# Gathers into one tile, weighted sums behind the attention heads, and PSUM copies pinned to ScalarE, in a two-layer recurrent, mixture-of-experts and attention kernel

## The chip, the cores and the metric

The kernel runs as one program on 1 core of one Trainium2 chip. The metric is the time of the execution on the device in microseconds, the median over several runs. Short names: PE is TensorE (PEld its weight loads), DVE is VectorE, ACT is ScalarE, POOL is GpSimd, SP is SyncE, which here only issues DMAs.

## The reference, cut to what matters

The input has 8 batches of 512 tokens with 128 channels, 4096 tokens in all. Everything is float32. Two layers follow each other, and each is `x + s * silu(g)` with two branches `s` and `g` over the same layer-normed input.

```python
# layer 0
xn = layernorm(x)
s  = mamba(xn) -> rmsnorm(+xn) -> gelu MLP -> rmsnorm          # scan over 512 tokens, 256 channels x 16 states
g  = silu(layernorm(moe24(relu(layernorm(moe24(xn)))) + xn))   # 24 experts, top-2, two passes
x  = x + s * g
# layer 1
xn = layernorm(x)
s  = attention(xn)        # 8 heads, causal over 512 tokens, head width 128
e1, e2 = top2(softmax(xn @ wg))                   # 128 experts, at most 32 rows each
yb = rows of xn sorted by expert @ we             # 2 x 4096 rows of 128
y  = w1[:, None] * yb[row1] + w2[:, None] * yb[row2]
x  = x + s * silu(y)
```

The last four lines matter most here. The second mixture of experts needs the routing of all 8 batches before its first expert can run, and every token then fetches two rows of the table `yb`, weights them and adds them.

## The kernel before

The work is written as Python generators, and the framework puts the instructions of each engine into a fixed order when the program is built. It goes by its own model of times and by the data dependences. Each engine then runs its list strictly in order. Semaphores make it wait for the other engines.

**Stage A (to about 690 us).** The first mixture of experts runs (`expert1`, `between`, `expert2`), interleaved with the first batches of the state-space model. One batch of the model is `front`, 8 steps of `scan` with 2 states each, `gate`, `gated` and `back`. The scan is DVE work: `L665` multiplies, `L667` is the scan proper and `L668` multiplies again. ACT makes `da` (`L663`), PE sums the products by transposing them into `py` (`L689`).

**Stage B (about 690 to 1309 us).** The attention of batches 0 to 5 (`EARLY = 6`) runs head by head beside the remaining batches of the model; the loop spreads the model's steps evenly over the 48 heads. For batch `b`, `fetch(b)` loads the layer-0 branches and adds gathered expert rows on POOL, and `after(b)` makes the input of layer 1: layernorm, a weight and a bias (`L605`, `L606`), silu (`L607`), times `s` (`L608`), plus `x` (`L609`). `prepare(b)` makes the transposed input `xaT`; `choose(b)` and `route(b)` rank the experts and scatter rows into `xs_dram` (`L896`).

One head is `probabilities` and then `values`. PE multiplies (`L914`, `L922`), DVE masks and takes the minimum (`L924`), ACT takes the exponential (`L928`), PE transposes the probabilities into one PSUM tile `pp` with a single buffer (`L942`), a copy takes them to `pT` in SBUF (`L944`), PE multiplies with `v` (`L949`) and DVE divides by the row sum and adds to `s1` (`L954`, `L958`, `L960`). The ten 128x128 blocks of a head go through `pp` in three groups: two of 128x384 and one of 128x512. Before heads 0 and 4 of a batch, `values_of` makes `v` for four heads: PE multiplies, and four copies of 128x512 bring it from PSUM (`L908`). Both kinds of copy are written for either engine:

```python
nc.any.tensor_copy(v[:, j, :, 0:D], pv)                      # L908
nc.any.tensor_copy(pT[:, first : first + n, :], pp[:, :n, :])  # L944
```

With `nc.any` the framework picks DVE or ACT for each copy when it builds the program.

**Stage C (about 1309 to 1400 us).** `back(7)` ends the model: the last `s`, in the tile `xo` (named `xnb` in the trace), is stored to `s_dram` (`L763`). `fetch(7)` loads it again as `sb` (`L583`), and `after(7)`, `prepare(7)`, `choose(7)` follow. The pools of the late stages (`psl`, `r3`, `mo`) are opened ahead of `after(7)`.

**Stage D (about 1400 to 1457 us).** `slots(t)` loads the sorted rows and transposes them into `xsT` (`L1025`, `L1028`, `L1030`), and `experts(e0)` multiplies them (`L1041`), masks them (`L1043`) and stores them to `yb_dram` (`L1044`). These steps are interleaved with the 16 late heads of batches 6 and 7 through the list `second`.

**Stage E (about 1457 us to the end).** `finish(b)` gathers two rows for each token from `yb_dram`: 8 indirect DMAs of 128 rows for a batch, 64 in all, issued by POOL (`L129`), into small tiles `ya`, `yc` with 6 buffers. DVE weights and adds them (`L1058`, `L1059`), ACT takes silu (`L1060`), DVE multiplies with the attention result `s1f` (`L1061`), adds `x1f` (`L1062`), and SP stores the batch. `finish(0)` to `finish(5)` stand in the list between the remaining heads, `finish(6)` and `finish(7)` behind them.

Of the kernel before, what the change touches and what calls it, by code (L numbers as in the profile page):

```python
# [8 lines left out]
F32 = mybir.dt.float32  # L9
# [11 lines left out]
P = 128  # L21
# [26 lines left out]
def tile_kernel(ctx: ExitStack, tc: tile.TileContext, t: dict, out: bass.AP):  # L48
# [94 lines left out]
    def rows(ap):  # L143

        return ap.rearrange("(j p) d -> p j d", p=P)
# [414 lines left out]
    def expert2(e, w):  # L560
# [14 lines left out]
            S.activation(os[:r, c, :], po[:r, c, :], AF.Copy, scale=wsl[:r, c, e : e + 1])  # L575
        store(os_dram, e, os)

    def fetch(b):

        o = af.tile([P, NJ, D], F32, name="o", bufs=2)  # L580
        Q.dma_start(o, rows(xn_dram[b * L : (b + 1) * L, :]))
        sb = af.tile([P, NJ, D], F32, name="sb")
        Q.dma_start(sb, rows(s_dram[b][:, :]))  # L583
# [12 lines left out]
        return o, sb, xb, o2  # L596

    def after(b, o, sb, xb, o2):

        E = G  # L600
        if o2 is not None:
            E = V
            V.tensor_tensor(o, o, o2, ALU.add)
        layernorm(st, o, o, NJ, eps6, "lno")
        E.tensor_tensor(o, o, bc(lno_w.unsqueeze(1), (P, NJ, D)), ALU.mult)  # L605
        E.tensor_tensor(o, o, bc(lno_b.unsqueeze(1), (P, NJ, D)), ALU.add)  # L606
        S.activation(o, o, AF.Silu)  # L607
        E.tensor_tensor(o, o, sb, ALU.mult)  # L608
        E.tensor_tensor(xb, o, xb, ALU.add)  # L609
        Q.dma_start(rows(x1_dram[b][:, :]), xb)  # L610
        return xb
# [111 lines left out]
    def back(b, yt):  # L723

        yz = mb.tile([P, 2, L], F32, name="yz")
        for hf in range(2):
            pt = ps_m.tile([P, L], F32, name="pyz", tag="pm")
            for i in range(NJ):
                T.transpose(pt[:, i * P : (i + 1) * P], yt[:, i, hf * P : (hf + 1) * P], ident)
            S.copy(yz[:, hf, :], pt)  # L730
        xo = mb.tile([P, NJ, D], F32, name="xnb")
        Q.dma_start(xo, rows(xn_dram[b * L : (b + 1) * L, :]))
        pr = ps_m.tile([P, NJ, D], F32, name="pr", tag="pm")
        for j in range(NJ):
# [28 lines left out]
        Q.dma_start(rows(s_dram[b][:, :]), xo)  # L763
        yield


# [35 lines left out]
    class Attention:  # L802
# [97 lines left out]
        def values_of(self, xaT, c):  # L900

            ps_q, pq = self.ps_q
            v = self.at.tile([P, NJ, 4, D + 1], F32, name="v", bufs=3)
            G.memset(v[:, :, :, D : D + 1], 1.0)
            for j in range(NJ):
                pv = ps_q.tile([P, 4, D], F32, name="pv1", tag=pq)
                T.matmul(pv, xaT[:, j * P : (j + 1) * P], self.w_vo[:, 4 * c : 4 * c + 4, :], start=True, stop=True)
                nc.any.tensor_copy(v[:, j, :, 0:D], pv)  # L908
            return v

        def probabilities(self, xaT, hd):
# [20 lines left out]
        def values(self, hd, prob, v, s1):  # L932
            at, (ps_t, pt), (ps_o, tpo) = self.at, self.ps_t, self.ps_o
            pT = at.tile([P, 10, P], F32, name="pT", bufs=2)
            for group in ((0, 1), (2,), (3,)):
                first = group[0] * (group[0] + 1) // 2
                n = sum(i + 1 for i in group)
                pp = ps_t.tile([P, NJ, P], F32, name="pp", tag=pt)
                c = 0
                for i in group:  # L940
                    for k in range(i + 1):
                        T.transpose(pp[:, c, :], prob[i][:, k * P : (k + 1) * P], ident)  # L942
                        c += 1
                nc.any.tensor_copy(pT[:, first : first + n, :], pp[:, :n, :])  # L944
            for i0 in range(0, NJ, 2):
                po = ps_o.tile([P, 2, D + 1], F32, name="po1", tag=tpo)
                for i in range(i0, i0 + 2):
                    for k in range(i + 1):
                        T.matmul(  # L949
                            po[:, i - i0, :], pT[:, i * (i + 1) // 2 + k, :], v[:, k, hd % 4, :],  # L950
                            start=(k == 0), stop=(k == i),
                        )
                rs = st.tile([P, 2], F32, name="rsum", bufs=4)
                V.reciprocal(rs, po[:, :, D])  # L954
                for i in range(i0, i0 + 2):
                    so, r = s1[:, i, :], rs[:, i - i0 : i - i0 + 1]
                    if hd == 0:
                        V.tensor_scalar(so, po[:, i - i0, 0:D], r, None, ALU.mult)  # L958
                    else:
                        V.scalar_tensor_tensor(so, po[:, i - i0, 0:D], r, so, ALU.mult, ALU.add)  # L960

        def heads(self, b, xaT):
            s1 = self.at.tile([P, NJ, D], F32, name="s1", bufs=2)
# [79 lines left out]
        V.tensor_tensor(yb, py, bc(live[:, e0 // 2 : e0 // 2 + 4].unsqueeze(2), (P, 4, D)), ALU.mult)  # L1043
        Q.dma_start(rows(yb_dram[2 * C1 * e0 : 2 * C1 * (e0 + 8), :]), yb)  # L1044

    def finish(b):
        s1 = mo.tile([P, NJ, D], F32, name="s1f")
        Q.dma_start(s1, rows(s1_dram[b][:, :]))
        x1 = mo.tile([P, NJ, D], F32, name="x1f")
        Q.dma_start(x1, rows(x1_dram[b][:, :]))  # L1050
        y = mo.tile([P, NJ, D], F32, name="y", tag="y")
        for j in range(NJ):
            i = b * NJ + j
            ya = mo.tile([P, D], F32, name="ya", tag="row", bufs=6)
            yc = mo.tile([P, D], F32, name="yc", tag="row", bufs=6)
            gather(ya, yb_dram, row1[:, i, 0:1])
            gather(yc, yb_dram, row1[:, i, 1:2])
            V.tensor_scalar(ya, ya, w121[:, i, 0:1], None, ALU.mult)  # L1058
            V.scalar_tensor_tensor(y[:, j, :], yc, w121[:, i, 1:2], ya, ALU.mult, ALU.add)  # L1059
        S.activation(y, y, AF.Silu)  # L1060
        V.tensor_tensor(y, y, s1, ALU.mult)  # L1061
        V.tensor_tensor(y, y, x1, ALU.add)  # L1062
        Q.dma_start(rows(out[b * L : (b + 1) * L, :]), y)


# [12 lines left out]
    def model():  # L1078
# [6 lines left out]
        for b in range(B):  # L1085
# [9 lines left out]
            for k in range(DS // NC):  # L1095
# [4 lines left out]
                    next(ending, None)  # L1100
                if k in (4, 5):
                    state = next(coming, None)
                if k == 6:
                    zsb = gate(xT)
                yield
            py, zs = pyb, zsb
# [72 lines left out]
        pass  # L1179
    for _ in attention_steps:  # L1180
        pass
    psc.close()
    ssm.close()

# [9 lines left out]
    xsT = r3.tile([P, E1, 2, C1], F32, name="xsT")  # L1194
    live = r3.tile([P, E1 // 2], F32, name="live")
    loaded = {e0: load_experts(e0) for e0 in range(0, 32, 8)}
    last = Attention(at, m_qk, w_vo, (ps_x, "px"), (ps_q, "pq"), (ps_s, "ps"), (ps_t, "pt"), (ps_o, "po"))
    for b in range(EARLY + 1, B):
        ready[b] = last.prepare(b, after(b, *fetch(b)))
        last.choose(b)  # L1200
    weights2()
    places()
# [12 lines left out]
    for t16 in range(E1 // 16):  # L1215
        second.append([lambda t16=t16: run_experts(t16)])
        if t16 + 1 < E1 // 16:
            second[-1].append(lambda t16=t16: slots(t16 + 1))
    for b in range(EARLY):
        second.append([lambda b=b: finish(b)])  # L1220
    for _ in late():
        for f in second.pop(0) if second else []:
            f()
    for f in sum(second, []):
        f()
    for b in range(EARLY, B):
        finish(b)
    psl.close()
    atc.close()

# [63 lines left out]
```

## Time and profile before

| what | value |
|---|---|
| time, median of 7 runs (lowest to highest) | 1554.15 us (1545.77 to 1561.83) |
| the profiled execution: its time, its span | 1553.7 us, 1552.0 us |
| mean granted TensorE clock | 0.894 |
| busy: PE, PEld | 1224.5 us (79%), 861.0 us (55%) |
| busy: DVE, ACT, POOL | 1240.6 us (80%), 971.4 us (63%), 582.6 us (38%) |
| DMA: bytes, mean rate | 218.83 MB, 141 GB/s |
| chain that ended last | DVE 39%, PE 28%, DMA 12%, issue 9%, ACT 6%, POOL 5% |

The span runs from the first to the last instruction of the core; 1.7 us of the execution's time lie outside it. Busy shares are means over stages with different limits, so the stages are read one by one. The chain is followed backward from the last instruction, at each step to what released it or to the instruction before it on its engine. The notation `[5.26 <-DMA s1f<-s_dram]` behind an instruction says that its engine stood idle for 5.26 us before it and that this DMA ended the wait. A name such as `L944` is a line of the kernel before; the diff shifts later lines of the changed kernel.

### The profile page before, as it was taken

How to read it: one execution, taken by the hardware profiler on the slowest of the kernel's cores; microseconds unless marked ns; L12 is line 12 of the kernel's file. 1: busy time of each engine (PE TensorE's matmuls, PEld its weight loads, DVE VectorE, ACT ScalarE, POOL GpSimd, SP SyncE). 2: the span in 40 equal slices, each digit the busy share in tenths (PEclk: the TensorE clock that was granted, in tenths of full speed). 3: DMA queues.
4: the chain of work that ended last, by engine and by line, in shares of the span. 5: the costliest groups of instructions: out<-in, count | busy, mean ns of one | idle time of the engine just before them, and what ended most of it. 6: DMA issues, size and time to landing. Idle time of an engine off the chain costs nothing.

```text
span 1552.0 us, 20556 instructions
## 1 busy us (share of the span) xinstructions
PE 1224.5 (79%) x6793; PEld 861.0 (55%) x6793; DVE 1240.6 (80%) x2789; ACT 971.4 (63%) x1670; POOL 582.6 (38%) x501
## 2 busy tenths in 40 slices
PE   6878798214489798467998998789889899898874
PEld 4544454214377777444566756656567567567543
DVE  5698677798857867988999999999899986475555
ACT  5356776585658677465868577477576664552453
POOL 1166552556155433654343025142600312020375
PEclk9689899555689999777999999999999899999978
DMA  6578777787377674543132223222311210338343
GB/s 185 178 241 273 231 240 258 231 259 255 122 244 224 207 218 143 140 109 88 58 102 68 72 94 82 75 65 72 94 57 55 64 54 13 89 86 248 109 133 99
DMA packets 170220, 218.83 MB, mean 141 GB/s; under 512 B 16618, under 2 KB 117562, under 8 KB 170114
## 3 DMA queue, kind: packets, MB, share of 16 engines
q1 hardware_dynamic: 126018, 99.39, 20.9%
q10 hardware_dynamic: 18432, 67.12, 13.0%
q0 software_dynamic: 25664, 51.01, 12.5%
q8 instruction: 54, 0.88, 0.2%
q14 instruction: 52, 0.43, 0.1%
HBM read 161.56 MB, written 55.84 MB: 140 GB/s over the span
## 4 chain that ended last, share of the span: by engine, by line
DVE 39%; PE 28%; DMA 12%; issue 9%; ACT 6%; POOL 5%; SPq 0%; ACTq 0%; DVEq 0%; POOLq 0%
DVE u L667 12%; DVE u L668 6%; DVE u L665 4%; PE po L949 4%; PE sc L922 3%; DVE sc L924 3%; PE py L689 2%; PE pc L621 2%; DVE s L960 2%; PE po L574 2%; PE pp L942 2%; DMA bb<-xd_dram 2%; PE ph L505 2%; DMA yc<-yb_dram,row 2%; DMA hd<-hs_dram,row 2%
## 5 line engine op out<-in xcount | busy, mean ns | idle before, releaser
L667 DVE TENSOR_TENSOR_SCAN u<-da,u 128x512 f32<-128x512 f32 x256 | 310.4, 1234 | 54.3 <-ACT da L663 54.2
L689 PE MATMUL py<-ident,u 128*128 128x128 f32 x1024 | 164.6, 302 | 153.0 <-DVE u L668 152.6
L689 PEld LDWEIGHTS py<-ident,u 128*128 128x128 f32 x1024 | 130.5, 155 | 199.5 <-DVE u L668 184.3
L949 PE MATMUL po<-v,pT 128*128 128x129 f32 x1280 | 185.2, 288 | 24.0 <-DVE s L960 16.8
L663 ACT ACTIVATE da<-dt,a_neg 128x512 f32<-128x512 f32 x256 | 176.9, 720 | 38.2 <-DVE u L667 33.3
L949 PEld LDWEIGHTS po<-v,pT 128*128 128x128 f32 x1280 | 168.4, 200 | 56.3 <-issue 33.9
L922 PE MATMUL sc<-xaT,qm 128*128 128x128 f32 (+3 forms) x512 | 182.6, 464 | 20.2 <-ACT prob L928 18.5
L928 ACT ACTIVATE prob<-sc,mn 128x128 f32<-128x128 f32 (+3 forms) x256 | 129.9, 527 | 90.9 <-DVE mn L924 81.9
L665 DVE TENSOR_TENSOR u<-bb,lp 128x1024 f32<-128x1024 f32 x128 | 154.6, 1229 | 16.5 <-DMA bb<-xd_dram 16.3
L668 DVE TENSOR_TENSOR u<-u,cb 128x1024 f32<-128x1024 f32 x128 | 157.9, 1234 | 1.2
L924 DVE CUSTOM_DVE_ANT_0 sc<-sc,mask 128x128 f32<-128x128 f32 (+3 forms) x256 | 124.6, 496 | 28.7 <-PE sc L922 26.5
L942 PE MATMUL pp<-ident,prob 128*128 128x128 f32 x640 | 112.8, 288 | 29.1 <-DVE pT L944 20.2
L132 POOL DMA_INDIRECT o<-os_dram,row x60 | 101.1, 1685 | 80.1 <-DMA o<-xn_dram 33.0
L129 POOL DMA_INDIRECT hg<-hid_dram,inv x72 | 92.7, 1287 | 95.1 <-PE pht L569 66.1
L942 PEld LDWEIGHTS pp<-ident,prob 128*128 128x128 f32 x640 | 80.4, 147 | 85.9 <-issue 34.9
L896 POOL DMA_INDIRECT xs_dram<-xn,idx x64 | 78.3, 1223 | 130.1 <-DVE row L893 50.8
L129 POOL DMA_INDIRECT xg<-xn_dram,inv x72 | 93.2, 1295 | 80.1 <-PE px L498 49.2
L922 PEld LDWEIGHTS sc<-xaT,qm 128*128 128x128 f32 x512 | 84.0, 199 | 64.2 <-ACT prob L928 39.7
L129 POOL DMA_INDIRECT hd<-hs_dram,row x64 | 76.5, 1196 | 69.9 <-ACT xs L622 23.2
L944 ACT COPY pT<-pp 128x384 f32<-128x384 f32 (+1 forms) x105 | 53.9, 513 | 62.3 <-PE pp L942 53.6
L574 PE MATMUL po<-we,hgT 128*128 128x128 f32 (+1 forms) x576 | 79.9, 286 | 0.9 <-ACT hgT L571 0.8
L574 PEld LDWEIGHTS po<-we,hgT 128*128 128x128 f32 (+1 forms) x576 | 71.3, 189 | 15.4 <-issue 10.3
(307 smaller groups left out, 2527.4 us busy)
## 6 DMA issues: line engine op xcount, KB each, us to landing
bb<-xd_dram ACTq DMA_DIRECT2D x64, 512.0 KB
cb<-xd_dram ACTq DMA_DIRECT2D x64, 512.0 KB
we<-in_W SPq DMA_DIRECT2D x48, 256.0 KB
hs_dram<-hs SPq DMA_DIRECT2D x24, 512.0 KB
hid_dram<-hd SPq DMA_DIRECT2D x32, 256.0 KB
we<-in_we SPq DMA_DIRECT2D x16, 512.0 KB
hs_dram<-hs SPq DMA_DIRECT2D x24, 192.0 KB
xb<-in_x SPq DMA_DIRECT2D x16, 256.0 KB
```

What stands on the lines that cost most here:

```text
L129: G.indirect_dma_start(dst, None, table[:, :], IOA(idx, 0))
L574: T.matmul(po[:r, c, :], hT[:, f, :r], we[:, f, :], start=False, stop=(f == NJ - 1))
L663: S.activation(da[:, j, :], dt[:, hf, :], AF.Exp, scale=a_neg[:, hf, n0 + j : n0 + j + 1])
L665: V.tensor_tensor(u, bb, bc(dx[:, hf : hf + 1, :], (P, NC, L)), ALU.mult)
L667: V.tensor_tensor_scan(u[:, j, :], da[:, j, :], u[:, j, :], 0.0, ALU.mult, ALU.add)
L668: V.tensor_tensor(u, u, cb, ALU.mult)
L689: T.matmul(py[:, i, hf * P : (hf + 1) * P], us[hf][:, j, i * P : (i + 1) * P], ident, is_transpose=True, start=False, stop=(n0 + j == DS - ...
L922: T.matmul(sc[:, :w], qm[:, i * P : w], xaT[:, :w], start=True, stop=True)
L924: V.tensor_tensor_reduce(sc[:, :w], sc[:, :w], mask[:, L - w :], -1.0, FMAX, ALU.add, ALU.min, mn[:, i : i + 1])
L928: S.activation(pr, sc[:, :w], AF.Exp, bias=mn[:, i : i + 1], scale=-1.0)
L942: T.transpose(pp[:, c, :], prob[i][:, k * P : (k + 1) * P], ident)
L949: T.matmul(po[:, i - i0, :], pT[:, i * (i + 1) // 2 + k, :], v[:, k, hd % 4, :], start=(k == 0), stop=(k == i),)
```

## The change

1. **Copies of `v`**: all 64 go to ACT (`S.copy`) instead of `nc.any`.
2. **Copies of transposed probabilities**: the 64 widest, 128x512, go to ACT; the 128 of 128x384 stay with `nc.any`.
3. **Gathers**: all 64 write into one tile `yr`, which takes the place of `xsT` in SBUF (same tag), and are issued as one entry of the list `second`.
4. **Weighted sums**: `finish(b)` for all batches is written behind the heads. It multiplies the 128x1024 elements of a batch in one DVE instruction and adds the halves in another. `follows` puts the first of them behind the last head's `summed` on DVE and keeps at most two batches open at a time. The buffers of `s1f` and `x1f` go from 2 to 3.
5. **The last batch's `s`** stays in SBUF: no store to `s_dram` and no load; `after(7)` uses the tile `xo` itself, runs its four elementwise steps on DVE instead of POOL, and is written ahead of the late pools.
6. **The last batch's `gate`** comes at scan step 2 instead of step 6.

```diff
@@ fetch
-        sb = af.tile([P, NJ, D], F32, name="sb")
-        Q.dma_start(sb, rows(s_dram[b][:, :]))
+        sb = None
+        if b < B - 1:
+            sb = af.tile([P, NJ, D], F32, name="sb")
+            Q.dma_start(sb, rows(s_dram[b][:, :]))
@@ after
-        E = G
+        E = V if b in (0, B - 1) else G
         if o2 is not None:
-            E = V
             V.tensor_tensor(o, o, o2, ALU.add)
+        sb = last_s[0] if sb is None else sb
@@ back
-        Q.dma_start(rows(s_dram[b][:, :]), xo)
+        if b < B - 1:
+            Q.dma_start(rows(s_dram[b][:, :]), xo)
+        else:
+            last_s.append(xo)
@@ values_of
-                nc.any.tensor_copy(v[:, j, :, 0:D], pv)
+                S.copy(v[:, j, :, 0:D], pv)
@@ values
-                nc.any.tensor_copy(pT[:, first : first + n, :], pp[:, :n, :])
+                if n == NJ:
+                    S.copy(pT[:, first : first + n, :], pp)
+                else:
+                    nc.any.tensor_copy(pT[:, first : first + n, :], pp[:, :n, :])
...
-                        V.scalar_tensor_tensor(so, po[:, i - i0, 0:D], r, so, ALU.mult, ALU.add)
+                        self.summed = V.scalar_tensor_tensor(so, po[:, i - i0, 0:D], r, so, ALU.mult, ALU.add)
@@ finish
-    def finish(b):
-        s1 = mo.tile([P, NJ, D], F32, name="s1f")
+    def outputs():
+
+        yr = r3.tile([P, B, NJ, 2, D], F32, name="yr", tag="xsT")
+        for b in range(B):
+            yield yr[:, b]
+            for j in range(NJ):
+                for k in range(2):
+                    gather(yr[:, b, j, k, :], yb_dram, row1[:, b * NJ + j, k : k + 1])
+
+    finished = []
+
+    def finish(b, yr):
+        s1 = mo.tile([P, NJ, D], F32, name="s1f", bufs=3)
...
+        weighted = V.tensor_tensor(yr, yr, bc(w121[:, b * NJ : (b + 1) * NJ, :].unsqueeze(3), (P, NJ, 2, D)), ALU.mult)
+        follows(weighted, last.summed)
+        if b >= 2:
+            follows(weighted, finished[b - 2])
         y = mo.tile([P, NJ, D], F32, name="y", tag="y")
-        for j in range(NJ):
-            i = b * NJ + j
-            ya = mo.tile([P, D], F32, name="ya", tag="row", bufs=6)
-            yc = mo.tile([P, D], F32, name="yc", tag="row", bufs=6)
-            gather(ya, yb_dram, row1[:, i, 0:1])
-            gather(yc, yb_dram, row1[:, i, 1:2])
-            V.tensor_scalar(ya, ya, w121[:, i, 0:1], None, ALU.mult)
-            V.scalar_tensor_tensor(y[:, j, :], yc, w121[:, i, 1:2], ya, ALU.mult, ALU.add)
+        V.tensor_tensor(y, yr[:, :, 0, :], yr[:, :, 1, :], ALU.add)
@@ model
-                if k == 6:
+                if k == (6 if b < B - 1 else 2):
                     zsb = gate(xT)
@@ tail of the program
+    gate_of = {b: after(b, *fetch(b)) for b in range(EARLY + 1, B)}
     psc.close()
     ssm.close()
...
-        ready[b] = last.prepare(b, after(b, *fetch(b)))
+        ready[b] = last.prepare(b, gate_of[b])
...
-    for b in range(EARLY):
-        second.append([lambda b=b: finish(b)])
+    got = []
+    second.append([lambda: got.extend(outputs())])
     for _ in late():
         for f in second.pop(0) if second else []:
             f()
-    for f in sum(second, []):
-        f()
-    for b in range(EARLY, B):
-        finish(b)
+    for b in range(B):
+        finish(b, got[b])
```

More of the change, by code (lines that the diff above doesn't have):

```diff
@@ L576, in expert2 @@
         store(os_dram, e, os)
+    last_s = []
     def fetch(b):
@@ L957, in values @@
                     if hd == 0:
-                        V.tensor_scalar(so, po[:, i - i0, 0:D], r, None, ALU.mult)
+                        self.summed = V.tensor_scalar(so, po[:, i - i0, 0:D], r, None, ALU.mult)
                     else:
-                        V.scalar_tensor_tensor(so, po[:, i - i0, 0:D], r, so, ALU.mult, ALU.add)
+                        self.summed = V.scalar_tensor_tensor(so, po[:, i - i0, 0:D], r, so, ALU.mult, ALU.add)
         def heads(self, b, xaT):
@@ L1044, in experts @@
         Q.dma_start(rows(yb_dram[2 * C1 * e0 : 2 * C1 * (e0 + 8), :]), yb)
-    def finish(b):
-        s1 = mo.tile([P, NJ, D], F32, name="s1f")
+    def outputs():
[8 more added lines that the diff above has]
+        s1 = mo.tile([P, NJ, D], F32, name="s1f", bufs=3)
         Q.dma_start(s1, rows(s1_dram[b][:, :]))
-        x1 = mo.tile([P, NJ, D], F32, name="x1f")
+        x1 = mo.tile([P, NJ, D], F32, name="x1f", bufs=3)
         Q.dma_start(x1, rows(x1_dram[b][:, :]))
+        weighted = V.tensor_tensor(yr, yr, bc(w121[:, b * NJ : (b + 1) * NJ, :].unsqueeze(3), (P, NJ, 2, D)), ALU.mult)
+        follows(weighted, last.summed)
+        if b >= 2:
+            follows(weighted, finished[b - 2])
         y = mo.tile([P, NJ, D], F32, name="y", tag="y")
-        for j in range(NJ):
-            i = b * NJ + j
-            ya = mo.tile([P, D], F32, name="ya", tag="row", bufs=6)
-            yc = mo.tile([P, D], F32, name="yc", tag="row", bufs=6)
-            gather(ya, yb_dram, row1[:, i, 0:1])
-            gather(yc, yb_dram, row1[:, i, 1:2])
-            V.tensor_scalar(ya, ya, w121[:, i, 0:1], None, ALU.mult)
-            V.scalar_tensor_tensor(y[:, j, :], yc, w121[:, i, 1:2], ya, ALU.mult, ALU.add)
+        V.tensor_tensor(y, yr[:, :, 0, :], yr[:, :, 1, :], ALU.add)
         S.activation(y, y, AF.Silu)
         V.tensor_tensor(y, y, s1, ALU.mult)
-        V.tensor_tensor(y, y, x1, ALU.add)
+        finished.append(V.tensor_tensor(y, y, x1, ALU.add))
         Q.dma_start(rows(out[b * L : (b + 1) * L, :]), y)
@@ L1193, in tile_kernel @@
     mo = pool(psl, "mo", 2, "left")
-    xsT = r3.tile([P, E1, 2, C1], F32, name="xsT")
+    xsT = r3.tile([P, E1, 2, C1], F32, name="xsT", tag="xsT")
     live = r3.tile([P, E1 // 2], F32, name="live")
```

## Prediction, made before the changed kernel ran

> **What bounds the kernel now.** I read the busy times by stage first, because the mean shares (PE 79%, DVE 80%) mix stages with different limits. Columns: stretch, length, busy us (instructions) of PE, PEld, DVE, ACT and POOL, granted clock, DMA share, GB/s.
>
> ```profile
> 700.00:1000.00 300.00, 271.91 (x1441) 186.08 (x1442) 287.56 (x725) 204.58 (x324) 92.66 (x69) 0.95 0.27 79
> 1000.00:1309.00 309.00, 274.14 (x1472) 191.21 (x1470) 282.69 (x735) 200.35 (x341) 80.79 (x62) 0.94 0.21 62
> 1309.00:1344.00 35.00, 30.12 (x157) 20.12 (x157) 15.04 (x46) 20.44 (x45) 9.18 (x10) 1.00 0.08 23
> 1344.00:1360.00 16.00, 15.85 (x69) 9.56 (x69) 7.94 (x35) 10.95 (x20) 2.53 (x2) 1.00 0.89 229
> 1360.00:1400.00 40.00, 38.06 (x224) 26.94 (x222) 32.71 (x140) 24.69 (x47) 7.95 (x9) 1.00 0.30 80
> 1400.00:1457.00 57.00, 51.35 (x459) 39.63 (x460) 30.05 (x74) 16.59 (x33) 0.00 (x0) 0.97 0.79 222
> 1457.00:1552.00 95.00, 55.83 (x265) 39.55 (x263) 51.70 (x173) 43.16 (x64) 61.78 (x64) 0.84 0.37 103
> ```
>
> In stage B (the first two rows, 609 us) DVE is busy for 570 us and idle for 39; PE is busy for 546, ACT for 405. DVE leads with PE close behind. In C and D PE is nearly full, and in E no engine is. Following the chain of work piece by piece from 690 to 1310 us, I count 350 us of DVE and 174 of PE. Of the DVE part, 18.8 us are copies to `pT` and 5.4 copies to `v`.
>
> The groups by shape give the copies that the change moves, and the waits show how PE fares with either engine.
>
> ```profile
> L908 DVE COPY v<-pv x35: 659/678/692, 704.0 to 1472.2; 128x512 f32<-128x512 f32 x35
> L908 ACT COPY v<-pv x29: 566/585/606, 694.5 to 1476.3; 128x512 f32<-128x512 f32 x29
> L944 ACT COPY pT<-pp x105: 458/479/592, 717.9 to 1538.3; 128x384 f32<-128x384 f32 x69, 128x512 f32<-128x512 f32 x36
> L944 DVE COPY pT<-pp x87: 516/552/692, 714.5 to 1535.8; 128x384 f32<-128x384 f32 x59, 128x512 f32<-128x512 f32 x28
> PEld pp L942 <- ACT pT L944: 7.7, 17, 1.8
> PEld pp L942 <- DVE pT L944: 9.6, 12, 1.7
> ```
>
> ACT is the quicker copier (585 against 678 ns), and PE loses about as little behind ACT's copies (7.7 us in 17 waits in B) as behind DVE's (9.6 in 12).
>
> The timeline shows the last batch's `s` going out to DRAM and back.
>
> ```profile
> 1343.15 1.14 DVE L721 SCALAR_TENSOR_TENSOR xnb<-zm,rms_ss,n1w 128x128 f32<-128x128 f32 x4
> 1344.31 0.36 SPq L763 DMA_DIRECT2D s_dram<-xnb  x1
> 1350.78 1.74 SPq L583 DMA_DIRECT2D sb<-s_dram  x1
> 1357.25 1.27 POOL L608 TENSOR_TENSOR o<-o,sb 128x512 f32<-128x512 f32 x1 [26.17 <-DMA sb<-s_dram]
> 1358.60 1.26 POOL L609 TENSOR_TENSOR xb<-o,xb 128x512 f32<-128x512 f32 x1
> ```
>
> Stage E is a line of gathers on POOL, from the first to the last, and then the last sums:
>
> ```profile
> 1457.56 0.99 POOL L129 DMA_INDIRECT ya<-yb_dram,row  x1 [59.86 <-DMA yb_dram<-yb]
> 1459.33 0.95 POOL L129 DMA_INDIRECT yc<-yb_dram,row  x1 [0.78 <-issue]
> 1538.08 0.94 POOL L129 DMA_INDIRECT yc<-yb_dram,row  x1 [0.30 <-issue]
> 1540.93 0.35 DVE L1059 SCALAR_TENSOR_TENSOR y<-yc,w,ya 128x128 f32<-128x128 f32 x1 [1.25 <-DMA yc<-yb_dram,row]
> 1541.40 0.61 DVE L960 SCALAR_TENSOR_TENSOR s<-po,rsum,s 128x128 f32<-128x128 f32 x2
> 1547.27 0.69 DVE L1061 TENSOR_TENSOR y<-y,s1f 128x512 f32<-128x512 f32 x1 [5.26 <-DMA s1f<-s_dram]
> ```
>
> POOL issues one gather every 1.25 us without a gap, 64 in 80.5 us. Six buffers cost nothing there. The last head ends at 1542.0, 1.2 us behind the last gather's landing, and its result then goes out and in again before the final sums.
>
> **The copies (stage B).** In the order in which the two programs are built, up to the last `yt` (L709), DVE loses 28 copies of `v` (28 x 0.678 = 19.0 us) and 24 wide ones (24 x 0.69 = 16.6). It gains 4 narrow ones that `nc.any` moves back (4 x 0.55 = 2.2) and L605 and L606 of batch 7 (2 x 0.69 = 1.4): 32 us less. ACT gains 28 x 0.585 + 24 x 0.58 - 4 x 0.48 = 28 us, on top of 405 in 609, and so stays under 72%. That cover holds unless a copy has to queue (second rival). What follows for the time is bounded by 32 us (DVE sets every microsecond) and 0 (PE takes over at once; its 546 us then exceed DVE's 538). The nearest row is the chain: 5.4 us of `v`, and of the 18.8 for `pT` the wide share, 16.6 / (16.6 + 48 x 0.55) = 39%, 7.3 us: 12.7 together. The new order also has 174 ACT table loads instead of 190, 16 x 1.28 = 20 us less on ACT, of which little lies on the chain (5.1 us there are the loads of L928). I take 15 us.
>
> On table loads the row is 1283 ns, and the next activation starts at once (load at 1310.97, L928 at 1312.26). The Trainium skill ("ScalarE: Activation LUTs", What ACT_TABLE_LOAD costs) adds a drain of some 1.38 us to each switch. By the page ACT would win an estimated 16 x 2.66 = 43 us instead of 20; this trace shows no such drain.
>
> **The last batch's `s` and `gate` (C and D).** After `xnb` at 1344.29 the chain needs store, load and two POOL steps until L107 starts at 1359.90: 15.6 us. In the new order two DVE steps of 0.69 us follow directly, about 1.5 us, with nothing queued ahead of them but a 0.29 us reduction: 14 us less on the path to the routing. SP loses one store and one load; the expert weights queued there (L1034) move up. `yt` started at 1309.18 after `zs` at 1308.55, while PE had ended `py` at 1300.6; with `gate` four scan steps earlier up to 8 us could go, but choosing experts for batch 6 fills that time, so I count 4.
>
> But PE did not idle meanwhile: 15.85 of 16 us. It ran late heads, which must run somewhere. In the old order 5.7 heads lie between the end of `back(7)` and the first `slots`, and 3.3 from there to the last expert; in the new one 3.2 and 5.1. An undisturbed head costs 6.4 us of PE (about 2.2 for L949, 1.1 for L942, 2.2 for L922, 0.9 for L914). So stage D takes on 1.8 x 6.4 = 11.5 us of PE work, of which its 5.6 idle us cover a part at best: D grows by some 8. Net 14 + 4 - 8 = 10 us, between 2 (nothing covered, no gate) and 18 (all covered, since D also moves 222 GB/s and may wait for its transfers anyway).
>
> **Gathers and sums (E).** 64 gathers stay 64, so 84 us from the last `yb` store's landing (1456.8) to the last gather's (1540.84) stay. DVE loses 32 x 0.286 + 32 x 0.35 = 20 us that stood between the heads, with waits for gathers in front of them (14.9 us for `yc`, 13.0 for `ya`). Heads therefore run at their own pace: 7.7 remain behind the last expert (7.0 before), at the 6.9 us from one head's first division to the next's in stage C (L954 at 1384.70 and 1391.58), 53 us. Then 8 sums of 1.23 (as L665, 128x1024) + 3 x 0.69 = 3.3 us wait, 26 us: ready at 79, before the last gather at 84. The end is the last batch: in the new order its DVE steps are shared with batch 6, so 1.23 + 0.69 + 0.83 for a silu and its hand-over + 5 x 0.69 = 6.2 us, then 3.3 us for the store as before (1548.71 to 1552.0). 84 + 6.2 + 3.3 = 93.5 instead of 95.2: 2 us, between 0 and 4. ACT's one silu table load falls before the gathers end.
>
> Two of 64 gathers took 1.41 us instead of 0.94, both beside sums of L1061 and L1062; beside the sums of the five other batches that were summed during the gathers none did. So 2 of 14 such steps cost 0.47 us, and the 32 DVE steps of the new sums cost at most 32 x 2/14 x 0.47 = 2 us by these rows, which the end from 0 to 4 covers.
>
> The Trainium skill ("SBUF — State Buffer", SBUF: two separate sides) says that a DVE instruction with two SBUF inputs locks a port against a GpSimd operation that reads SBUF, for its whole length. If descriptor making counted, the gathers would lose an estimated 26 us and this change would lose all it won; the rows above speak against that.
>
> **The sum.** 15 + 10 + 2 = 27 us from the profiled execution's 1553.7 us (span 1552.0, and 1.7 outside) gives 1527. That execution lies 0.45 us under the median, so the same number stands for the median.
>
> **Rivals.** *PE sets the pace of B.* For: 546 busy us against DVE's 538 afterwards, and 95% busy in parts. Against: the chain has twice as much DVE as PE. B gives nothing, 1542 (1537 to 1549).
>
> *ScalarE's queue holds the copies.* `pp` has one buffer, so a copy behind an exponential (0.53 us), a `da` (0.72) or a table load (1.28) stops PE's next transposes. If each of the 52 copies moved in B waits 0.47 us longer and DVE's relief is lost, 24 - 12 gives 1566. It decides from 12 / 52 = 0.23 us per copy. Against: the two wait rows above.
>
> *Everything DVE sheds counts.* 32 + 18 + 4: 1500.
>
> *The heads stay slow.* At the 11.4 us per head that batch 7 has now (8 heads from 1449.8 to 1541.2), they end 88 us after the last store, and 26 + 3 us of sums and store follow: 22 us worse there, about 1551 in all.
>
> **Chances.** Forecast 0.52 (own range 1512 to 1539), PE 0.20, all counts 0.10, ScalarE's queue 0.13, slow heads 0.05. About 0.5%, 7.8 us, is what a measurement can tell here: faster below 1546.4, slower above 1561.9. A quarter of the PE case and of the ScalarE case, and the slow heads, fall between, so faster 0.77, same 0.13, slower 0.10. The range 1500 to 1560 leaves out half of "all counts" and three quarters of the ScalarE case, 0.15.
>
> **What would show it.** Right: DVE busy under 545 us between 700 and the last `yt`, that `yt` some 15 to 19 us earlier, L107 within 2 us of `xnb`, gathers still every 1.25 us, heads over 25 us before the end. Wrong: PE waits for ACT's `pT` copies well over 0.3 us each, stage D longer than 70 us, or sums still queued on DVE when the last gather lands.

## The result, and the profile after

The changed kernel takes 1573.31 us (median of 15 runs, 1562.44 to 1583.71), the kernel before 1555.75 us (36 runs, 1540.48 to 1565.43). The ratio is 1.0108, 95% interval 1.0085 to 1.0131: 17 us slower, where 27 us faster was forecast, and outside the range of 1500 to 1560.

The profiled execution has a span of 1573.2 us against 1552.0. Four events, read from the two timelines, cut the 21.2 us into stages:

| event | before | after | stage ending there: change |
|---|---|---|---|
| last `yt` starts (L709, now L713) | 1309.2 | 1323.9 | +14.7 |
| first scatter of the last batch into `xs_dram` | 1387.5 | 1396.0 | -6.2 |
| first gather from `yb_dram` | 1457.6 | 1477.5 | +11.4 |
| end of the span | 1552.0 | 1573.2 | +1.2 |

Each trace is one execution. The control of the fourth group below keeps the order and the engines of the kernel before, and its last `yt` starts at 1313.9, 4.7 us later; so a difference of some 5 us between two traces says little by itself.

The busy times of the changed kernel by stage, with the same columns as in the prediction:

```profile
700.00:1000.00 300.00, 257.93 (x1335) 175.25 (x1335) 274.14 (x694) 214.53 (x343) 96.41 (x72) 0.94 0.27 78
1000.00:1324.00 324.00, 283.97 (x1550) 199.39 (x1549) 276.65 (x699) 212.22 (x371) 74.62 (x57) 0.93 0.21 61
1409.00:1477.00 68.00, 66.35 (x552) 50.50 (x551) 38.43 (x108) 25.38 (x49) 0.13 (x1) 1.00 0.65 185
```

In stage B DVE is now busy for 550.8 of 624 us instead of 570 of 609, at nearly the same granted clock (0.94 and 0.93 against 0.95 and 0.94). So DVE did lose work, and idles 73 us instead of 39; the stage has become longer, not shorter. In stage D PE is full (66.35 of 68 us).

The copies went where the change sent them (groups by shape). The waits from 690 to 1324 us show both new and longer ones. `L952` is the widest copy, which is pinned; `L954` is the copy of 128x384, which the framework still places:

```profile
L952 ACT COPY pT<-pp 128x512 f32<-128x512 f32 x64 | 37.4, 584 | 23.5 <-PE pp L949 22.9
L915 ACT COPY v<-pv 128x512 f32<-128x512 f32 x64 | 36.7, 587 | 19.3 <-PE pv L914 19.1
PEld pp L949 <- DVE pT L954: 19.9, 13, 7.2
PEld pp L949 <- ACT pT L954: 10.0, 15, 5.3
PEld po L959 <- ACT pT L952: 5.4, 7, 2.1
DVE lno_st L107 <- DMA o<-os_dram,row: 16.0, 5, 7.3
```

The last of these rows, of the kernel before:

```profile
DVE lno_st L107 <- DMA o<-os_dram,row: 5.2, 1, 5.2
```

PE's weight loads of the transposes now wait 19.9 us for DVE's remaining copies (9.6 before for all of DVE's), with one wait of 7.2 us. DVE itself stood still ahead of them: at `L107` of `after` it waits 16.0 us for gathered rows (5.2 before), once for 7.3 us, and copies of 128x384 stand behind that step in its list. For the pinned widest copies PE hardly waits with its next transposes (0.4 us in all); it waits with the multiplication that reads `pT` (5.4 us).

The timeline of stage C shows the last batch's `s` without its way through DRAM:

```profile
1366.67 1.14 DVE L725 SCALAR_TENSOR_TENSOR xnb<-zm,rms_ss,n1w 128x128 f32<-128x128 f32 x4
1367.84 0.69 DVE L612 TENSOR_TENSOR o<-o,xnb 128x512 f32<-128x512 f32 x1
1369.39 0.46 DVE L107 BATCH_NORM_STATS2 ln_st<-xb 128x6 f32<-128x128 f32 x2
```

L107 starts 1.6 us behind `xnb`; it was 15.6 us. And stage E:

```profile
1524.85 0.61 DVE L970 SCALAR_TENSOR_TENSOR s<-po,rsum,s 128x128 f32<-128x128 f32 x2
1555.63 1.43 POOL L129 DMA_INDIRECT yr<-yb_dram,row  x1 [0.30 <-issue]
1561.12 0.94 POOL L129 DMA_INDIRECT yr<-yb_dram,row  x1 [0.30 <-issue]
1563.81 1.23 DVE L1072 TENSOR_TENSOR yr<-yr,w 128x1024 f32<-128x1024 f32 x1 [6.83 <-DMA yr<-yb_dram,row]
```

The heads end 48 us before the end, and DVE waits for gathers, as forecast.

### The profile page after: what moved, and what is told of

The parts are those of the page before. It is cut to its first block, busy times and chain, and to the rows that moved or that the text cites. A ratio compares the mean times of both kernels' runs of the same rounds, so it can differ in the third digit from the quotient of the medians.

```text
span 1573.2 us, 20450 instructions
## 1 busy us (share of the span) xinstructions
PE 1214.4 (77%) x6793; PEld 853.3 (54%) x6793; DVE 1219.7 (78%) x2688; ACT 979.3 (62%) x1711; POOL 589.4 (37%) x497
## 3 DMA queue, kind: packets, MB, share of 16 engines
q10 hardware_dynamic: 18432, 67.12, 12.7%
## 4 chain that ended last, share of the span: by engine, by line
DVE 31%; PE 30%; POOL 11%; DMA 10%; issue 10%; ACT 7%; SPq 0%; ACTq 0%; POOLq 0%; DVEq 0%
DVE u L671 10%; DVE u L672 5%; PE sc L929 4%; POOL yr L129 4%; PE po L959 4%; DVE u L669 3%; PE py L693 2%; DMA hd<-hs_dram,row 2%; POOL xs_dram L903 2%; POOL o L132 2%; DVE sc L931 2%; PE pp L949 2%; PE po L574 2%; DMA bb<-xd_dram 2%; PE ph L505 2%
## 5 line engine op out<-in xcount | busy, mean ns | idle before, releaser
L693 PEld LDWEIGHTS py<-ident,u 128*128 128x128 f32 x1024 | 133.8, 158 | 204.1 <-DVE u L672 185.6
L935 ACT ACTIVATE prob<-sc,mn 128x128 f32<-128x128 f32 (+3 forms) x256 | 132.1, 529 | 102.7 <-DVE mn L931 95.0
L929 PE MATMUL sc<-xaT,qm 128*128 128x128 f32 (+3 forms) x512 | 179.2, 459 | 19.5 <-ACT prob L935 15.1
L959 PE MATMUL po<-v,pT 128*128 128x129 f32 x1280 | 178.3, 284 | 13.0 <-DVE s L970 7.5
L959 PEld LDWEIGHTS po<-v,pT 128*128 128x128 f32 x1280 | 163.7, 197 | 39.8 <-issue 13.7
L132 POOL DMA_INDIRECT o<-os_dram,row x60 | 105.1, 1752 | 78.8 <-DMA o<-xn_dram 32.7
L949 PE MATMUL pp<-ident,prob 128*128 128x128 f32 x640 | 109.3, 283 | 24.5 <-DVE pT L954 18.0
L129 POOL DMA_INDIRECT xg<-xn_dram,inv x72 | 97.5, 1353 | 80.1 <-PE px L498 49.5
L929 PEld LDWEIGHTS sc<-xaT,qm 128*128 128x128 f32 x512 | 82.1, 196 | 62.3 <-ACT prob L935 36.1
L129 POOL DMA_INDIRECT hd<-hs_dram,row x64 | 81.6, 1275 | 65.9 <-DMA qkv_w<-in_qkv_w 23.6
L129 POOL DMA_INDIRECT yr<-yb_dram,row x64 | 64.8, 1013 | 78.4 <-ACT pT L954 58.7
```

The lines of the kernel that those rows point to most:

```text
L129: G.indirect_dma_start(dst, None, table[:, :], IOA(idx, 0))
L132: G.indirect_dma_start(dst, None, table[:, :], IOA(idx, 0), compute_op=ALU.add)
L693: T.matmul(py[:, i, hf * P : (hf + 1) * P], us[hf][:, j, i * P : (i + 1) * P], ident, is_transpose=True, start=False, stop=(n0 + j == DS - ...
L929: T.matmul(sc[:, :w], qm[:, i * P : w], xaT[:, :w], start=True, stop=True)
L959: T.matmul(po[:, i - i0, :], pT[:, i * (i + 1) // 2 + k, :], v[:, k, hd % 4, :], start=(k == 0), stop=(k == i),)
```

## The experiments

0.1% of the time is 1.55 us. Ratios are to runs of the kernel before on the same chip (its median there was between 1550 and 1555 us, and 1582 us in the third group), with 95% intervals. On the chip of the third group the line of 64 gathers is 94 to 97 us long in the four traces, elsewhere 80 to 84.

**First group: which part of the change.**

The copies alone (on the kernel before):

```diff
-                nc.any.tensor_copy(v[:, j, :, 0:D], pv)
+                S.copy(v[:, j, :, 0:D], pv)
...
+                if n == NJ:
+                    S.copy(pT[:, first : first + n, :], pp)
+                else:
+                    nc.any.tensor_copy(pT[:, first : first + n, :], pp[:, :n, :])
```

> The kernel before with parts 1 and 2 alone: all copies of v and the widest copies of transposed probabilities on ScalarE. Theory A (the copies, with the order that is built around them, lose time in the stage with the scan and the attention): the last yt comes 10 to 17 us later than in the kernel before (about 1320), the stages behind it keep their lengths, about 1568 us. Theory B (the changes at the end do the harm: gate earlier, after(7) on DVE, heads pushed among the experts): the copies alone give what the prediction said, the last yt 10 to 15 us earlier, about 1540. Theory C (both lose): last yt 3 to 8 us later, about 1560.

Measured: 1573.52 us, ratio 1.0137 (1.0099 to 1.0176), last `yt` at 1323.4. Theory A, even beyond its number: the copies alone lose what the whole change loses. But only 14.2 us of the trace's loss lie ahead of the last `yt`; the stages behind it do not all keep their lengths, as the theory had it. From the first gather to the end 101.3 us pass instead of 94.4, and the last heads end 91.4 us behind the first gather instead of 84.5.

Parts 3 to 6 without the copies (the changed kernel with both copies as `nc.any`):

> The changed kernel with both kinds of copy left to the framework again: parts 3 to 6 alone. Theory A: the last yt near 1309 as before, the scatter of the last batch 15 us earlier in relation to it, stage D 8 to 12 us longer, about 1548. Theory B: the last yt near 1320 and stage D near 69 us, 1565 to 1572. Theory C: about 1562.

Measured: 1548.47 us, ratio 0.9987 (0.9961 to 1.0014), last `yt` at 1299.1, first scatter at 1372.1 (15.4 us earlier than before), first gather at 1452.0 (5.5 us earlier). So the routing is ready 15 us sooner, and stage D gives 10 of them back. The time is that of theory A, the way to it is not: 10.1 of the 15.4 us lie ahead of the last `yt`, which theory A had at 1309, and only 5.3 behind it. Why the `yt` comes sooner no run shows. 1.0137 x 0.9987 = 1.0124, near the 1.0108 of the whole change, so the two halves add up in the total. By stage they do not: added, they put the last `yt` 4.1 us later and lengthen stage E by 7.1, where the changed kernel has 14.7 and 1.2.

The changed kernel with the gate back:

```diff
-                if k == (6 if b < B - 1 else 2):
+                if k == 6:
```

> The changed kernel with the last gate back at scan step 6. Theory A: the gate hardly matters, 1570 to 1576, the last yt 1320 to 1327. Theory B with the early gate as its cause: the early gate puts batch 7's projection and its rms chain in front of the scan's multiplications; then the last yt returns to 1309 to 1312 and the time to about 1560.

Measured: 1563.64 us, ratio 1.0068 (1.0040 to 1.0097). The last `yt` stays at 1325.5, against theory B, yet the time falls by some 6 us (the two intervals overlap a little), against theory A: the gate costs behind the `yt`. From there to the first scatter 63.1 us pass, in the changed kernel 72.2. PE's timelines show how, first of the changed kernel, then with the gate back:

```profile
1328.30 0.27 PE L887 MATMUL plc<-cnt,tri_b 32*128 32x256 bf16 x1 [0.56 <-DVE cnt L881]
1330.53 3.62 PE L921 MATMUL pqm<-xaT,m_qk 128*128 128x512 f32 x4
1335.23 0.82 PE L733 MATMUL pyz<-ident,yt 128*128 128x128 f32 x5
```

```profile
1327.14 1.04 PE L733 MATMUL pyz<-ident,yt 128*128 128x128 f32 x8
```

With the early gate, PE's list has the routing of batch 6 (L887) and the projection of a head (L921) in front of the transposes of `yt`; they start 10.1 us behind the end of `yt` (1325.1), instead of 0.4.

The gathers and sums alone (parts 3 and 4 on the kernel before):

> The kernel before with parts 3 and 4 alone: all gathers into one tile and the sums behind the heads. Up to the first expert the order of work is that of before, so nothing up to about 1450 us should move. Prediction's step for stage E: 2 us faster (0 to 4), about 1553. Rival (the sums lose by being last: the silu table load and six dependent steps stand behind the last gather): 1 to 3 us slower. In both the first gather starts within 2 us of before, and the heads end more than 20 us before the end.

Measured: 1553.48 us, ratio 1.0009 (0.9978 to 1.0041); first gather at 1458.1, end of the last head at 1503.8. Neither a gain nor a loss that can be measured.

**Second group: engine or order.** The framework orders each engine's instructions anew when the copies are pinned. Of the 2378 numbered DVE instructions in the built program with the copies alone, 1664 stand in the old sequence, of PE's 4782, 3927. The numbering of instructions is the same in both, so a kernel can carry another's lists as edges without semaphores:

```diff
+    def as_it_stood():
+        for text in STOOD.values():                 # one list for each engine
+            names = ["I-%d" % n for n in unpack(text)]
+            for a, b in zip(names, names[1:]):
+                tc.add_manual_dep(nc.get_inst_by_name(b), a, NoSync, reason="order")
```

Copies on ScalarE, lists of the kernel before:

> All copies of v and the widest copies of transposed probabilities on ScalarE, as in the run with the copies alone, but every engine keeps the order in which the kernel before was built (its lists are written into the kernel as edges; only the 63 copies that change their engine stand where the framework puts them on ScalarE). The run with the copies alone took 1573.5, the kernel before 1550.4. Theory 'order' (the framework's new order around the copies loses the time, the copies themselves are harmless or a gain): at most 1552, and if the prediction's 15 us for the copies are real, 1530 to 1540. Theory 'engine' (the copies wait on ScalarE's queue and hold up PE): 1565 to 1575. Between them: both have a share.

Copies on VectorE, lists of the run with the copies alone:

> The opposite: every engine keeps the order that was built for the run with the copies alone, but the 63 copies go back to VectorE. Theory 'order': slower than 1565, and if VectorE's 35 us come on top where it leads, 1575 to 1600. Theory 'engine': back near 1550 to 1558.

| | old order | order built for the copies |
|---|---|---|
| the 63 copies on VectorE | 1 (the kernel before) | 1.0329 (1.0289 to 1.0369) |
| the 63 copies on ScalarE | 1.0065 (1.0040 to 1.0089) | 1.0137 (1.0099 to 1.0176) |

The two columns differ in one thing more: when it built the new order, the framework also gave 42 of the 128 copies of 128x384 to the other engine (63 are on VectorE instead of 59), and these runs keep that. "Order" stands for both.

Both theories hold a part. With every list kept, the move alone costs 10 us; the order built for it costs another 11. Within that order the copies are better on ScalarE (by 30 us), so the order suits the move, and still the pair is worse than the old pair. In the traces the move with the old lists costs 9.0 us ahead of the last `yt` and nothing behind the first gather (93.9 us to the end, 94.4 before). The new order costs time in both places: behind the first gather 101.3 us with the copies on ScalarE and 102.0 with them on VectorE. The waits from 690 to 1309 us, of the kernel before (one line) and of the run with the old order (four):

```profile
DVE sc L924 <- PE sc L922: 11.2, 21, 1.8
```

```profile
DVE sc L962 <- PE sc L960: 36.1, 36, 6.5
PEld pp L980 <- ACT pT L154: 12.0, 18, 3.6
PEld pv L945 <- ACT v L151: 10.1, 8, 3.2
PEld po L987 <- ACT pT L154: 7.6, 5, 2.7
```

(The lists shift the lines: L154 and L151 are the copies, L962 is the mask.) From 690 to 1324 us PE and PEld wait 54.3 us for ScalarE's copies of `v` and `pT` instead of 13.4, and 23.2 us for VectorE's instead of 34.4 (the rows of both are added, so a wait that both show counts twice). PE hands the scores on later, and VectorE, relieved of the copies, waits for them: 36.1 us instead of 11.2. From the timelines I took the time between the end of a copy's last transpose and its start. For the widest copies in stage B:

| | count | mean wait |
|---|---|---|
| before, on ScalarE | 22 | 0.31 us (median 0.04) |
| before, on VectorE | 24 | 0.80 us |
| old order, all on ScalarE | 46 | 0.76 us |
| changed kernel, all on ScalarE | 46 | 0.77 us |

If the 22 kept their 0.31 us, the 24 that moved wait an estimated (46 x 0.76 - 22 x 0.31) / 24 = 1.17 us: longer than they had waited on VectorE.

How long PE stands still for them is another matter. The same sums of waits of PE and PEld, from 690 us to the last `yt` and split by the copy that ended them, with VectorE's own waits for the gathers of `fetch` in the last column:

| | for `v` and the widest `pT` | for `pT` of 128x384 on VectorE | VectorE for gathered rows |
|---|---|---|---|
| before | 16.2 us | 21.4 us | 5.2 us |
| old order, copies on ScalarE | 44.3 us | 23.3 us | 4.9 us |
| new order, copies on VectorE | 13.7 us | 40.0 us | 15.9 us |
| new order, copies on ScalarE | 13.3 us | 37.9 us | 16.1 us |
| changed kernel | 12.2 us | 39.5 us | 16.0 us |

So ScalarE's queue holds up PE where the old lists are kept. In the order that the framework built, and in the changed kernel, PE waits no longer for the moved copies than before; it waits for the copies of 128x384 that stayed on VectorE, and VectorE waits for gathered rows, on whichever engine the 63 copies are.

**Third group: which copies, and what the new order spoils.** Copies of `v` alone, and widest copies alone, with the old lists:

> The old order kept, and only the 35 copies of v that VectorE had go to ScalarE. With these and the 28 wide copies in the old order it took 1560.3, 9 us more than the kernel before. In that trace PE waits 26.8 us in all for ScalarE's copies of v (nearly nothing before) and 30.5 us for its copies to pT. Theory 'each in proportion to PE's waits': 1555. If the copies of v are harmless, as the prediction had it: at most 1551.

> The old order kept, and only the 28 widest copies to pT that VectorE had go to ScalarE. Theory 'each in proportion to PE's waits': 1555. If the wide copies are harmless and v costs all 9 us: at most 1552; if they carry it all: 1558 to 1562.

Measured: `v` alone 1.0027 (0.9996 to 1.0058), the widest alone 1.0069 (1.0035 to 1.0104). By the ratios the widest copies carry most of the loss, against the theory "in proportion"; for `v` the interval includes no loss. That the two do not add up exactly to 1.0065 is within the intervals. Why the widest cost more stays open: PE's waits are alike, 20.7 us for `v` in the one run and 23.3 for the widest in the other. The single buffer `pp` is not the main place: of the 23.3 us, 7.1 are transposes that wait for `pp`, and 16.2 are multiplications that wait for `pT`.

The order built for the copies, with seven steps of VectorE set back (L107 and those that depend on it, 3 to 23 places):

> The copies alone, in the order that was built for them (1573.5), except that seven layernorm steps of the layer-1 inputs, at which VectorE stood waiting for POOL's gathers or sums (20 us of such waits in the trace of the run with the copies alone), stand 3 to 23 places later on VectorE. Theory 'stalls at the head of VectorE's queue': most of these waits vanish, 1555 to 1565. Rival (PE and ScalarE would not have fed VectorE meanwhile, so other waits take their place): 1569 to 1575.

Measured: 1.0081 (1.0051 to 1.0112) instead of 1.0137. The waits of VectorE from 690 to 1324 us, with the copies alone and with the steps set back:

```profile
DVE rsum L957 <- PE po L952: 14.3, 14, 2.2
DVE lno_st L107 <- DMA o<-os_dram,row: 16.1, 5, 7.2
DVE ln_st L107 <- POOL xb L609: 6.6, 3, 3.8
```

```profile
DVE rsum L992 <- PE po L987: 20.4, 22, 2.8
DVE ln_st L127 <- POOL xb L647: 0.9, 1, 0.9
```

The waits for the gathers of `fetch` (16.1 us; 5.2 before the change) are gone and those for POOL's sum nearly so; of these 22 us, 6 come back at the row sums as a wait for PE. PE's waits for the copies of 128x384 on VectorE fall from 37.9 to 30.8 us. By the ratios the time falls by some 9 us, most of the 11 that the order costs; but the two intervals overlap a little, the runs are from different chips, and the last `yt` comes at 1322.7 instead of 1323.4. So the size of the gain is not settled.

VectorE's old list alone, the other engines free:

> All copies on ScalarE; only VectorE keeps the order of the kernel before, the other engines are ordered anew by the framework (PE's list agrees with the old one in 4208 of 4782 places instead of 3911). Theory 'VectorE's list is what the new order spoils': about 1560, as with all lists kept. Theory 'the new lists of PE and ScalarE carry the loss': 1568 to 1575.

Measured: 1.0197 (1.0163 to 1.0230), slower than both expectations. With the copies on ScalarE, VectorE's old list among new lists of the other engines is worse than either whole order (1.0065 and 1.0137). That speaks against VectorE's list as the only one that spoils the new order; the run does not say which others do.

**Fourth group: what VectorE's relief is worth.** In the old order the 63 copies stay on VectorE but take 8 of every 128 columns (and a control at full width):

```diff
+        if on == "s":
+            V.tensor_copy(dst[:, :, 0:8], src[:, :, 0:8])
```

> The old order kept. The 35 copies of v and 28 wide copies to pT that VectorE had in the kernel before stay on VectorE but take only 8 of every 128 columns (the rest of v and pT is left as it was in five tiles that are reused, so the outputs are not the reference's): VectorE loses some 35 us of work, and ScalarE gains nothing. If VectorE's work sets the time of the stage (the prediction's term, 15 of 32 us): 10 to 20 us faster than the control, ratio 0.987 to 0.994; then the copies' cost on ScalarE in the old order is that gain plus 9 us. If VectorE's relief is worth nothing there: within 4 us.

> The control of the run with narrow copies: the old order, all copies on the engines of the kernel before and in full width, but v and pT in the same five reused tiles. Same as the kernel before within 4 us.

Measured: 0.9935 (0.9907 to 0.9963), the control 0.9984 (0.9958 to 1.0009), within the 4 us expected. The groups of the run with narrow copies:

```profile
L153 DVE COPY v<-pv 128x32 f32<-128x32 f32 x35 | 6.2, 182 | 7.6 <-PE pv L963 7.5
L160 DVE COPY pT<-pp 128x32 f32<-128x32 f32 x28 | 5.1, 181 | 1.5 <-PE pp L998 1.5
```

Over the whole program VectorE loses 35 x (0.678 - 0.182) + 28 x (0.69 - 0.181) = 31.6 us of work, and the time falls by 8 us against the control, 10 against the kernel before. The relief is real, and in the old order worth a quarter to a third of its length, at or just under the low end of what was expected. With the copies on ScalarE the time is 1.0065 - 0.9935 = 1.3%, 20 us, above this run: that is what ScalarE's copies cost in the old order. In the new order moving them off VectorE gains 30 us, so what the same relief is worth depends on the order too.

**A version that beats both.** Parts 3 to 5, copies left to the framework, gate at step 6; and the same with the experts ahead of the heads:

```diff
     for _ in late():
-        for f in second.pop(0) if second else []:
-            f()
+        for _ in range(2):
+            for f in second.pop(0) if second else []:
+                f()
```

> Parts 3 to 5: the changed kernel with the copies left to the framework and the last gate at step 6. With the early gate it took 1548.5. If the early gate costs (on the changed kernel, undoing it won 10 us): 1538 to 1545. If the early gate only cost beside the pinned copies: 1547 to 1552.

> The same as the run with parts 3 to 5, but the list of late steps gives two of its entries for each head instead of one, so that 2.6 heads instead of 5.1 lie among the experts in PE's order and 10.2 instead of 7.7 behind them. Theory 'heads lengthen stage D' (68.7 us after, 57.2 before): D falls by up to 2.5 x 6.4 = 16 us, to about 53, and the heads still end before the last gather (10.2 x 6.9 = 70 us against 84): 10 to 15 us faster than the run with parts 3 to 5. Rival (D waits for its transfers of rows, weights and results): D stays above 62 us and the time within 3 us.

Measured: 1545.69 us, ratio 0.9964 (0.9935 to 0.9993), and 1533.97 us, 0.9882 (0.9833 to 0.9931). In the first, from the first `pxs` to the first gather 69.0 us pass (57.2 before the change, 68.8 after it), in the second 49.7, with its busy times in the experts' part:

```profile
1384.00:1430.00 46.00, 40.97 (x424) 33.54 (x425) 28.28 (x67) 12.05 (x23) 0.13 (x1) 1.00 0.92 257
```

PE has slack here (40.97 of 46 us), and the DMAs, 92% busy, are now the busiest part. The heads that were pushed back end at 1500, 16 us before the last gather is issued, so they cost nothing there.

## Why the prediction was wrong, point by point

**The copies: forecast 15 us faster, measured 21 us slower. This is the step that failed.** The copies left VectorE as counted (28 and 24 in stage B), but its busy time there fell by 19.4 us (570.2 to 550.8), not by 32. And what follows for the time was wrong in three things.

1. *"What follows for the time is bounded by 32 us ... and 0."* The lower bound was not one. It rested on "ACT ... stays under 72%. That cover holds unless a copy has to queue". A share says nothing of a queue: on ScalarE the moved copies began later behind their transposes than on VectorE (an estimated 1.17 us against 0.80 in the old order), and with every list kept the move cost 10 us instead of gaining.
2. *"PE loses about as little behind ACT's copies as behind DVE's."* The rows are right and were read wrongly. They hold both widths, and the copies that move are hardly in them: of the 7.7 us behind ACT 0.6 belong to the widest, of the 9.6 behind DVE 1.3. Before, the widest copies that the framework gave to ScalarE began 0.04 us (median) behind their transposes, so it gave them there mostly where ScalarE was free. The rows describe copies chosen for a free engine, not a copy that has to go there. The rival "ScalarE's queue" named the mechanism and a threshold of 0.23 us for each copy; it got 0.13 as its chance because of this reading. Its price, 24 us with the relief of 12 against it, stands beside 20 and 8 to 10 measured in the old order. It does not describe the changed kernel, though, where PE waits 12.2 us for the moved kinds of copy instead of 16.2: there the rival came near the time (1566 against 1573) without its mechanism.
3. *No term for the new order.* The prediction counted what the order moves at the end, but in stage B took from it only a saving in table loads, and that belongs to other parts: the copies alone have 189 loads, before there were 190. In the whole program 714 of 2378 VectorE instructions do not stand in the old sequence. The new order costs 11 us on top of the move. In stage B the traces with it show VectorE waiting 16 us for gathered rows instead of 5, and PE 38 to 40 us instead of 21 for the copies of 128x384 on VectorE; setting seven of VectorE's steps back removed those waits of VectorE and some of PE's. How the cost divides among the engines' lists stays open.

The relief itself, 15 us taken from 12.7 on the chain, was worth 8 to 10 in the old order. On table loads the changed kernel agrees with the row and not with the Trainium skill's drain ("ScalarE: Activation LUTs", What ACT_TABLE_LOAD costs): a load at 951.69 us takes 1.28, and L935 starts at 952.99.

**The last batch's `s`: forecast 14 us, measured 15.** From the last L761 (L765 after) to the first scatter 49.1 us passed before, 33.8 after. L107 follows `xnb` by 1.6 us, forecast within 2.

**The gate: forecast 4 us faster; the runs point to a loss.** 6 us on the changed kernel and 3.6 us without the pinned copies (0.9987 against 0.9964); the intervals of each pair overlap, but both point the same way and the trace shows the place. The prediction said that "choosing experts for batch 6 fills that time"; it fills PE's queue ahead of `yt`'s transposes.

**Stage D: forecast 8 us longer, measured 11.4.** The mechanism was right: with fewer heads in it the stage shrinks to 49.7 us. PE's busy time in it rose by 15.0 us (51.35 to 66.35), 3.5 more than the 11.5 counted, and its idle time of 5.6 us covered 4. The bound by which all is covered, because D waits for its transfers, did not apply: the DMA share fell from 0.79 to 0.65 and rises to 0.92 only with heads moved out.

**Gathers and sums: forecast 2 us, measured none.** The heads end 48 us before the end, at "over 25". But 8 of 64 gathers took 1.22 to 1.91 us instead of 0.94, all beside sums, and the line of gathers is 83.6 us long instead of 80.5. The prediction held at most 2 us for this, from 2 of 14 sums; it was 3.1, and took away the whole gain. With the gathers and sums alone 6 gathers took 1.30 to 1.76 us, and their line is 82.6 us long. The 26 us estimated from the Trainium skill's rule on the shared port ("SBUF — State Buffer", SBUF: two separate sides), for the case that descriptor making counts, do not appear in this trace.

**What would show it.** VectorE's busy time from 700 us to the last `yt` was to be under 545 us and is 550.8; the `yt` was to come 15 to 19 us earlier and comes 14.7 later; stage D over 70 us was to be a sign of error, and it is 68.8 from the first `pxs`. PE's waits for ScalarE's copies "well over 0.3 us each" came: 10.0 us in 15 waits, 0.67 us each, with the longest at 5.3. But all 15 are for copies of 128x384, which the framework placed, and not for the pinned ones.

## What to carry to other kernels

The waits behind copies that a framework places are the waits of the chosen ones; price a pinned copy by what stands in that engine's queue when it becomes ready, not by the waits of the copies that were put there. A change that pins engines also rebuilds the order, so test the two apart: keep the old lists and change the engine, then the reverse. What holds an engine up in the one order need not be what holds it up in the other. And work that has slack at the end (heads beside a line of gathers) should not stand in front of the step that starts that line.

## What the runs showed that was not expected

With the same 63 copies on VectorE the time is that of the kernel before or 1.0329 of it, depending on the order built around them (and the places of the 42 smaller copies that came with it), a larger effect than any part of the change. And of 31.6 us of work taken off the busiest engine, with no list changed, only 8 to 10 us came off the time, while in the new order moving the copies off it gained 30.
